# A planned four-layer graph network on one core: where the attention weights are turned, who issues the loads, and how the last layer's products are split

## The chip, the cores and the metric

The kernel runs on one core of a Trainium2 chip. The metric is the device time of one execution in microseconds; the kernel before took 2353.08 us (median of three runs, 2349.69 to 2353.46).

## What is computed

Four pre-norm layers over 128 graphs of 128 nodes with 256 features each, in float32, with a 0/1 adjacency matrix `adj` for every graph. Before every layer h = relu(layernorm(x)); the layer's result is added to x.

```python
# layer 0: gated graph network, three steps with the same GRU weights
for i in range(3):
    m = einsum('bnd,de->bne', h, weight[i])
    h = gru_cell(einsum('bst,bsd->btd', A, m), h, w_ih, w_hh, b_ih, b_hh)
x = x + h
# layer 1: relational convolution (with a 0/1 adj only relation 1 is present)
x = x + (adj == 1) @ h @ weight[0] + bias
# layers 2 and 3: graph attention
Wh = h @ W.T
e = leaky_relu(Wh @ a1 [:, None] + Wh @ a2 [None, :], 0.2), masked by adj
x = x + softmax(e) @ Wh
```

## The kernel before

**Groups.** The 128 graphs are worked through in 32 groups of G = 4 graphs (`group`, L918). A tile of a group holds 128 partitions by T = 512 columns of float32, which is one PSUM bank. Groups 0 to 29 treat their four graphs in one piece (`whole`); the last two are split into pairs and single graphs (SPLIT, SINGLE), to shorten the end.

**Layer 0.** `norm` takes statistics (L696), computes 1/sqrt on GpSimd (L722) and scales on ScalarE (L743). The features are turned, so that h stands with features on the partitions (`turn`, L478). Each of the three steps (`step`, L940) does the neighbour sum on TensorE (`gather`, L974), splits its operands into three parts (`forms`: a rounded part L955 or L957, a remainder L961 and their difference, `difference` L470, mostly on GpSimd), and multiplies them with split weights in fp32r passes (`products`, L992). Between the passes ScalarE or VectorE rescales the bank (L1005, L1011, L1013). The gates are finished by L1023, L1035, L1040, L1042, L1045 and L1048. After each step h is turned back. The last step's h is added to x by `residual` (L1078 to L1083); the planner puts each addition on VectorE or on GpSimd.

**Turning over DRAM.** `turn` lets VectorE transpose blocks of 32 by 32 (L490), stores the tile in a DRAM buffer (`give`, L493, on SP), and loads it back with blocks exchanged, in four transfers (`take`, L502, on SP). TENSOR names what is turned by TensorE instead; before it is empty.

**Layers 1 to 3.** `product` (L792) multiplies first with the adjacency or the attention weights (`sums`, L765) and then with the layer's weight. If the layer is in THIN and the group is not one of the last PLAIN = 2, the intermediate bank is split in three forms (L806 or L808, L811, L470) and the second product is made of fp32r passes (`passes`, L819) with one rescale (L828 or L830) before the third. Otherwise the bank is copied (`evict`, L461) and multiplied in plain f32 (`mix`, L775). Before, THIN is (1, 2): layer 3 is plain. In attention (`attend`, L1129) the scores e are built and masked (L1119, L1166, L1170, L1173), exponentiated (L1179), turned (`turn`, in whole groups) into eT, and eT enters `product`; L1210 adds the normalized result to x.

**Loads.** Every group loads x twice (`fetch`, L510, two transfers each time), adj twice (`load`, L529, and `again`, L522) and the transposed adj once (L1095), each by SP. The first weights are issued by ScalarE's queue, the others by SP (`weights`, L540). Results are stored by SP (L1220).

**Order of the work.** The order on every engine is written out ahead by a planner (`Plan.order`, L215). It holds for each operation an engine or a choice of engines, a planned duration (`act`, `dve`, `dma` and numbers in the calls), and what it depends on. It places the operation that can start first, and among the operations of an engine that can start within NEAR the one with the lowest rank. The rank is made of the group's turn (PERIOD per group), the length of the way that still follows, and an offset per stage and site (OFFSETS). AHEAD = 5 groups may be open at a time. Buffers are counted: 8 PSUM banks, 11 `big` tiles, 3 of x, 5 of adjacency and others. Engines run their own lists in order and wait on semaphores.

Of the kernel before, what the change touches and what calls it, by code (L numbers as in the profile page):

```python
# [18 lines left out]
P = 128  # L19
# [19 lines left out]
OWN = {"PE": 0, "ACT": 125, "DVE": 125, "POOL": 80, "SP": 2500, "ACTQ": 2500}  # L39
PERIOD = 29902  # L40
CLOSE = 7183
CLOSING = 2
SOON = -210
# [3 lines left out]
LINE, SPREAD = 0, -1000  # L47
GIVE = -400
TAKE = -2500
TENSOR = ()  # L50
BLOCK = 32
NEAR = 69
# [12 lines left out]
THIN = (1, 2)  # L65
# [11 lines left out]
def act(n, ptrs=0):  # L77
    return 50 + 95 * ptrs + 0.833 * n


def dve(n):
    return 68 + n / 0.96


def dma(kb):
    return 470
# [3 lines left out]
    0: (-70252, -12514, 2287, 8809, -26238, -146194, 10750, 55634, 30994, -54821, -2879, -215, -254,),  # L90
    1: (-77596, -18751, -40109, -33244, -13055, -53723, -68528, 1773, -34806, -135119, 879, -98768, 51856,
        44795, -64452, -2716,),
    2: (-95804, -20611, 70568, -66959, -6282, -38365, 6331, 7167, -87557, -120685, 144159, 0, -60172, 22200,
        253, 2907, 38047,),
    3: (-102445, -23990, 38859, 16506, -38395, -77755, 61821, 576, 58832, 37279, 38392, 48590, -137270, -161,
        -4329, 88294, -5659, -1511, -24936, -35483,),
    4: (9420, 6970, 96990, 45577, 14137, -3081, -28597, -108133, -850, -77398, -8748, -81, 24213, -39147,
        5274, -117520, -39070, 4328, 73461, 2677, -9322, 38218,),
    5: (-53063, -10484, 13614, 9709, -9223, 0, 86360, -49387, 3891, -79089, 22834, -12125, 42, -143071,
        -20815, -7001, 39402, 8197, 210921, 979, -8129, 55104, -109511, 178418, -171023, -17919, -45955,  # L100
        32785, 202299, 15929, -75290, -16189,),
    6: (-8401, 1876, 0, -2867, -17545, -54409, -177384, 6635, -4173, 16809, 64025, 1422, -41374, 3498, 7298,
        112681, -960, 0, -167733, 3047, -20901, 48681, -50794, 104147, -14530,),
    7: (2011, -43268, -7473, -2193, -13120, 17374, 10030, 24727, -8835, -59753, 29500, -32772, -10542,
        -85496, -6214, -47593, 4322, -5746, -43839, -101654, -3101, 9392, -18883,),
    10: (31340, 140410, 166041, 86764, 86271, -82403, 47762, 173067, 157481, -33091, 90840, -8460, 85813,),
    11: (-90811, -5747, -11338, -10756, 2168, -27498, -36330, -9110, 13623, -65824, 59954, -36485, 65854,
        102114, -39462, 10659,),
    12: (-88894, -2718, 120398, -47746, 16864, -33143, 17060, 25017, -58235, -111482, 170409, 89873, -65258,
        61044, 3422, 23111, 49690,),  # L110
    13: (-59071, 17894, 109447, 41927, -4268, -51312, 111328, 77067, 108356, 88471, 46360, 263340, -35253,
        23414, 79162, 211888, 10834, -10383, 74698, 67176,),
    14: (-32758, 12684, 122607, -43352, -20519, -34186, -56784, -88737, -18648, -122741, -24236, -29303,
        31876, -49287, -17477, -128202, -71886, 71670, 64769, 11212, -103569, -34527,),
    15: (-186417, -106904, -40789, -64266, -8033, -13445, 16411, -115394, -129609, -221523, -34547, -153159,
        -40482, -146129, -99541, -93701, -50044, 14115, 99121, -155460, -34394, 49772, -135635, 90451,
        -238640, -50117, -75732, -67304, 110359, -120923, -153053, -106347,),
    16: (90192, 31519, 28924, 59971, 13927, -108659, -126696, 35607, 7022, 44259, 134646, 83504, 72967,
        -71833, 139898, 214088, -4475, 66727, -178916, 46932, 84371, 67621, 13000, 119832, 93548,),
    17: (2011, -43268, -7473, -2193, -13120, 17374, 10030, 24727, -8835, -59753, 29500, -32772, -10542,  # L120
        -85496, -6214, -47593, 4322, -5746, -43839, -101654, -3101, 9392, -18883,),
    20: (-107741, -75380, -118420, -44708, -69924, -229335, -95079, 10513, -7484, 27055, -96949, -215, -254,),
    21: (-241039, -37443, -85617, -204164, -130954, -212658, -180409, -165567, -39823, -261311, -133885,
        -103620, -20641, -66103, -225402, -138454,),
    22: (-120431, -90137, 129948, -127092, 11177, -90000, -80347, -35815, -106293, -139261, 141530, -54256,
        -129233, 7860, -119111, 29072, 3576,),
    23: (-144176, -87227, -85789, 1378, -81324, -238467, -3162, -78700, 46997, -3871, 33809, 42358, -177604,
        -35904, -119077, -63937, -38348, -135903, -24936, -35483,),
    24: (-200969, -199448, -70412, -199813, -160146, -250664, -235592, -342997, -205357, -303708, -186137,
        -202706, -168399, -243146, -236370, -300082, -270699, -214705, -104544, 2677, -9322, 38218,),  # L130
    25: (-61251, -50204, -55609, -84828, -90010, 10545, -51986, -177143, -111208, -144284, 59013, -46623,
        -56779, -179794, -83802, -190091, -64080, -63359, 54466, -41363, -72589, -54011, -140205, 135055,
        -306980, -77123, -140787, 32785, 202299, 15929, -75290, -16189,),
    26: (-81589, -13318, 8156, -109205, -83353, -110277, -231535, -35494, -89897, 10694, 20288, -77730,
        -166910, -72981, -43136, 895, -48027, -102602, -242066, -114463, -91143, 43689, -72571, 104147,
        -14530,),
    27: (2011, -43268, -7473, -2193, -13120, 17374, 10030, 24727, -8835, -59753, 29500, -32772, -10542,
        -85496, -6214, -47593, 4322, -5746, -43839, -101654, -3101, 9392, -18883,),
# [235 lines left out]
def kernel(  # L374
# [49 lines left out]
    def build(general):  # L424
# [53 lines left out]
        def turn(nm, srcs, dst=None, w=None):  # L478
# [7 lines left out]
            for k, (src, r) in enumerate(srcs):  # L486
                part = chunk(f"part{nm}{k}")

                def within(src=src, part=part):
                    nc.vector.transpose(part.t, src())  # L490

                def give(k=k, part=part):
                    nc.sync.dma_start(out=swap.t[k * G : (k + 1) * G].rearrange("g p c -> p g c"),  # L493
                                      in_=part.t.rearrange("p (g c) -> p g c", g=G))

                op("DVE", dve(T) + 15, within, r=[r], w=[part])
                op("SP", 470, give, r=[part], w=[(swap, {k})], late=GIVE)
# [7 lines left out]
            op("SP", 470 * P // BLOCK, take, r=[swap], w=[w], late=TAKE)  # L505
# [3 lines left out]

        def fetch(gi, name, after=()):  # L510
            xt = Buf(xs, f"{name}{gi}")
            for g2 in range(G // 2):
                op("SP", dma(256), lambda g2=g2: nc.sync.dma_start(
                    out=xt.t[:, 2 * g2 : 2 * g2 + 2, :],
                    in_=x[ds(gi * G + 2 * g2, 2)].rearrange("g n d -> n g d")),
                   w=[(xt, {2 * g2, 2 * g2 + 1})], after=after)
            return xt
# [4 lines left out]
        def again(gi, after):  # L522
            ai = Buf(adjs, f"again{gi}")
            op("SP", dma(256), lambda: nc.sync.dma_start(
                out=ai.t.rearrange("p (g j) -> p g j", g=G),
                in_=adj[ds(gi * G, G)].rearrange("g i j -> i g j")), w=[ai], after=after)
            return ai

        def load(gi):  # L529
            xt, ai = fetch(gi, "x0_"), Buf(adjs, f"adj{gi}")  # L530
            op("SP", dma(256), lambda: nc.sync.dma_start(
                out=ai.t.rearrange("p (g j) -> p g j", g=G),
                in_=adj[ds(gi * G, G)].rearrange("g i j -> i g j")), w=[ai])
            state[gi] = xt, ai
# [383 lines left out]
        def group(gi):  # L918
# [21 lines left out]
            def step(i, hs, hT):  # L940
# [136 lines left out]
                for k, h in enumerate(hs_new if i == L - 1 else ()):  # L1077
                    def residual(eng, k=k, h=h):  # L1078
                        part = xt.t[:, :, k * P : (k + 1) * P]
                        (nc.gpsimd if eng == "POOL" else nc.vector).tensor_tensor(  # L1080
                            part, part, h.t.rearrange("p (g d) -> p g d", g=G), ALU.add)

                    op(("DVE", "POOL"), (dve(T), 1250), residual, r=[h], w=[(xt, set(range(G)))], port=True)  # L1083
# [3 lines left out]
            for i in range(L):  # L1087
# [7 lines left out]
            op("SP", dma(256), lambda: nc.sync.dma_start(  # L1095
                out=aiT.t.rearrange("p (g j) -> p g j", g=G),
                in_=adjT[ds(gi * G, G)].rearrange("g i j -> i g j")), w=[aiT], after=late)
# [12 lines left out]
            def attention(i, mask):  # L1110
# [4 lines left out]
                for g in range(G):  # L1115
# [9 lines left out]
                    op("DVE", 850, terms, r=[(hs[g // 2], {g}), ub[i]], w=[junk, (s, {("ei", g)})], port=True)  # L1125
# [159 lines left out]
```

## Time and profile before

| | |
|---|---|
| runs | 2353.08, 2349.69, 2353.46 us |
| profiled execution | 2353.06 us, its span 2351.2 us |
| L992, GRU products | 6912 instructions, means 396 and 393 ns |
| L974 and L765, neighbour sums | 3072 instructions, means 276 to 278 ns |
| L775, plain f32 second products | 576 instructions, means 380 and 407 ns |
| L819, fp32r passes | 1440 instructions, means 294 and 285 ns |
| L490, 32x32 turns on VectorE | 252 of h and 60 of e, means 697 and 693 ns |
| L1080, last h added | 47 on VectorE (870 ns), 13 on GpSimd (1315 ns) |
| loads issued by SP | x 128, adj 64, transposed adj 32, of 256 KB each |
| swap stores and loads issued by SP | 312 of 256 KB; 992 of 64 KB and 128 of 128 KB |
| DMA | 270.36 MB, mean 115 GB/s |

A row of the groups gives the line of the kernel, the engine, the operation, the tiles written and read, their shape, how many there were, their busy time and the mean of one. A matmul's duration reaches from its first row to its last result, so consecutive ones overlap. A row of waits gives the waiting engine and line, the engine and line it waited for, the sum in us, how many times, and the longest.

### The profile page before, as it was taken

The numbers are of one execution on the slowest core, as the hardware profiler recorded it, in microseconds if no ns is written. First come the engines' busy times: TensorE is split into PE (matmuls) and PEld (weight loads), VectorE is DVE, ScalarE is ACT, GpSimd is POOL, SyncE is SP. The second block draws the span as 40 slices with busy tenths as digits, with TensorE's granted clock in tenths as the row PEclk, the third lists the DMA queues.
The fourth block names the chain that finished last, engine by engine and source line by source line (L and its number), as shares of the span: only waits on it lengthen the run. The fifth ranks groups of instructions, "written<-read, shape, count | busy, mean of one in ns | idle before, by whom it ended". The sixth has DMA issues, their size and how long they took to land.

```text
span 2351.2 us, 39064 instructions
## 1 busy us (share of the span) xinstructions
PE 2291.9 (97%) x12137; PEld 1947.2 (83%) x12137; DVE 1978.2 (84%) x5405; ACT 1582.0 (67%) x3272; POOL 912.4 (39%) x729
## 2 busy tenths in 40 slices
PE   7999999999999999999999999999999999999997
PEld 6788888888888888888888888888888888788885
DVE  7858888888888888888888888888888888888887
ACT  6566676766676666666666766666766666666665
POOL 2334334443334443334343334343334343344421
PEclk9999999999999999999999999999999999999999
DMA  8535445555445455455455455455554555545431
GB/s 249 143 83 110 96 90 124 117 128 116 102 110 125 111 133 113 100 117 117 114 126 118 107 115 115 114 129 116 108 115 112 118 122 109 128 103 118 105 77 43
DMA packets 951273, 270.36 MB, mean 115 GB/s; under 512 B 677008, under 2 KB 939280, under 8 KB 951056
## 3 DMA queue, kind: packets, MB, share of 16 engines
q1 hardware_dynamic: 949968, 266.72, 50.0%
q8 instruction: 99, 1.62, 0.3%
q14 instruction: 118, 0.97, 0.2%
q10 hardware_dynamic: 1088, 1.05, 0.1%
HBM read 168.96 MB, written 98.69 MB: 114 GB/s over the span
## 4 chain that ended last, share of the span: by engine, by line
PE 64%; DVE 14%; DMA 10%; ACT 6%; SPq 4%; issue 3%; DVEq 0%; POOL 0%; ACTq 0%
PE bank L992 40%; PE bank L819 7%; PE bank L765 6%; PE bank L974 5%; PE bank L775 5%; DMA swap<-big 4%; SPq L502 4%; DMA big<-swap 3%; DVE junk L1119 3%; DVE form L961 2%; DMA wide<-swap 2%; ACT big L743 1%; DVE wide L1042 1%; DVE wide L1045 1%; DVE big L490 1%
## 5 line engine op out<-in xcount | busy, mean ns | idle before, releaser
L992 PE MATMUL bank<-form,wh_s 128*128 128x512 f32 x3456 | 953.4, 396 | 8.7 <-ACT bank L1005 4.6
L992 PE MATMUL bank<-form,wi_s 128*128 128x512 f32 x3456 | 944.0, 393 | 1.6 <-ACT bank L1013 0.9
L470 POOL TENSOR_TENSOR form<-form,form 128x512 fp32r<-128x512 f32 x383 | 517.7, 1362 | 800.4 <-DVE form L961 565.0
L992 PEld LDWEIGHTS bank<-form,wi_s 128*128 128x128 f32 x3456 | 644.1, 188 | 143.6 <-ACT bank L1013 3.1
L992 PEld LDWEIGHTS bank<-form,wh_s 128*128 128x128 f32 x3456 | 631.8, 188 | 151.5 <-ACT bank L1005 15.8
L1013 ACT ACTIVATE bank<-bank 128x512 f32<-128x512 f32 x448 | 255.4, 574 | 325.7 <-PE bank L992 324.4
L722 POOL TENSOR_TENSOR small<-small,nhalf 128x4 f32<-128x4 f32 (+2 forms) x140 | 142.2, 1020 | 408.8 <-DVE small L720 338.9
L1119 DVE CUSTOM_DVE_ANT_0 junk<-big,ub 128x256 bf16<-128x256 f32 x512 | 244.5, 478 | 14.2 <-ACT big L743 0.5
L743 ACT ACTIVATE big<-xs,small 128x256 f32<-128x256 f32 x384 | 200.1, 590 | 21.6 <-DVE small L726 12.2
L696 DVE BATCH_NORM_STATS2 small<-xs 128x6 f32<-128x256 f32 x512 | 190.0, 415 | 7.3 <-DMA xs<-in_x_dram 6.0
L470 POOL TENSOR_TENSOR cform<-cform,cform 128x512 fp32r<-128x512 f32 x120 | 155.2, 1294 | 96.2 <-DVE cform L811 83.0
L490 DVE STREAM_TRANSPOSE big<-wide 128x512 f32<-128x512 f32 x252 | 173.1, 697 | 4.0 <-ACT wide L743 2.3
L1035 DVE SCALAR_TENSOR_TENSOR bank<-big,bank 128x512 f32<-128x512 f32 x192 | 131.9, 690 | 48.5 <-PE bank L992 35.9
L955 ACT ACTIVATE form<-wide 128x512 fp32r<-128x512 f32 x179 | 109.2, 626 | 83.7 <-DMA wide<-swap 43.4
L1179 ACT ACTIVATE big<-big,small 128x128 f32<-128x128 f32 x256 | 99.8, 392 | 70.0 <-DVE small L1173 69.7
L1023 ACT ACTIVATE bank<-bank,b_rz 128x512 f32<-128x512 f32 x192 | 123.4, 655 | 34.0 <-PE bank L992 30.1
L1210 DVE SCALAR_TENSOR_TENSOR xs<-bank,small,xs 128x256 f32<-128x256 f32 x256 | 118.4, 475 | 31.6 <-PE bank L775 23.0
L1042 DVE TENSOR_TENSOR wide<-wide,bank 128x512 f32<-128x512 f32 x192 | 126.9, 682 | 21.4 <-ACT bank L1040 21.1
L765 PE MATMUL bank<-big,big 128*128 128x128 f32 x1024 | 130.7, 277 | 11.9 <-DVE wide L1045 7.1
L1023 ACT ACTIVATE big<-bank,b_rz 128x512 f32<-128x512 f32 x192 | 130.1, 681 | 16.3 <-PE bank L992 12.1
L765 PEld LDWEIGHTS bank<-big,big 128*128 128x128 f32 x1024 | 123.1, 192 | 19.4 <-DVE wide L1045 9.9
L974 PE MATMUL bank<-adjs,big 128*128 128x128 f32 x1024 | 131.2, 276 | 6.4 <-DMA big<-swap 5.1
(105 smaller groups left out, 3297.5 us busy)
## 6 DMA issues: line engine op xcount, KB each, us to landing
swap<-big SPq DMA_DIRECT2D x312, 256.0 KB, 2.5
big<-swap SPq DMA_DIRECT2D x992, 64.0 KB, 2.3
xs<-in_x_dram SPq DMA_DIRECT2D x128, 256.0 KB, 3.1
adjs<-in_adj_dram SPq DMA_DIRECT2D x64, 256.0 KB, 3.4
wide<-swap SPq DMA_DIRECT2D x128, 128.0 KB, 3.6
big<-line SPq DMA_DIRECT2D x60, 256.0 KB, 3.9
out_dram<-xs SPq DMA_DIRECT2D x30, 512.0 KB, 3.1
big<-in_adj_dram SPq DMA_DIRECT2D x32, 256.0 KB, 4.0
```

Source lines behind the costliest of these rows:

```text
L470: (nc.gpsimd if eng == "POOL" else nc.vector).tensor_tensor(at(df), at(lo).bitcast(F32), at(hi).bitcast(F32), ALU.subtract)
L490: nc.vector.transpose(part.t, src())
L696: op("DVE", dve(D), lambda g=g: nc.vector.bn_stats(s.t[:, ST + 6 * g : ST + 6 * g + 6], xt.t[:, g, :]), r=[(xt, {g})], w=[(s, {("mv", g)})])
L743: nc.scalar.activation(place(g), xt.t[:, g, :].rearrange("p (k m) -> p k m", k=KC), AF.Relu, bias=s.t[:, MR + g : MR + g + 1], scale=s.t[: ...
L765: nc.tensor.matmul(ps.t[:, (len(gs) * k + j) * P : (len(gs) * k + j + 1) * P], hs[g // 2].t[:, (g % 2) * D + k * P : (g % 2) * D + (k + 1) ...
L819: nc.tensor.matmul(po.t[:, j * D : (j + 1) * D], fs[f].t[:, (len(gs) * k + j) * P : (len(gs) * k + j + 1) * P], w.t[:, f, k, :], start=(st ...
L974: nc.tensor.matmul(pg.t[:, g * P : (g + 1) * P], of()[:, g * P : (g + 1) * P], flags(m0)[:, g * P : (g + 1) * P], start=True, stop=True,)
L992: nc.tensor.matmul(ps.t, w.t[(slice(None), *row, j, k, slice(c * P, (c + 1) * P))], b.t, start=(start and x == 0), stop=(x == len(terms) - ...
L1013: nc.scalar.mul(ps.t, ps.t, by)
L1023: op("ACT", act(T, 1), lambda: nc.scalar.activation(to.t, ps.t, AF.Tanh, bias=b_rz.t[:, c : c + 1], scale=0.5), r=[b_rz, *([ps] if kept el ...
L1042: op("DVE", dve(T), lambda c=c, ps=ps: nc.vector.tensor_tensor(hT.t[:, c, :], hT.t[:, c, :], ps.t, ALU.subtract), r=[ps], w=[(hT, {c})])
L1119: nc.vector.tensor_tensor_reduce(out=junk.t, in0=part, in1=ub[i].t[:, v, :], op0=ALU.mult, op1=ALU.add, scale=1.0, scalar=0.0, accum_out=s ...
```

## The change

- TENSOR becomes `("e",)`: in whole groups, too, the attention weights are turned by four TensorE transposes into a bank and copied out (`turn_all` and `evict`, which the last groups used before).
- A helper `arrive` issues the loads of x, adj and transposed adj by ScalarE (QUEUE = "ACT"), in ScalarE's own list of work.
- THIN becomes (1, 2, 3): layer 3's second product is made in three passes as well, with split weights.
- `residual` is always on GpSimd.
- The planner's durations, margins, PERIOD, CLOSE and all OFFSETS have other values, so the order of the work is another one.

```diff
-OWN = {"PE": 0, "ACT": 125, "DVE": 125, "POOL": 80, "SP": 2500, "ACTQ": 2500}
-PERIOD = 29902
-CLOSE = 7183
+OWN = {"PE": 0, "ACT": 125, "DVE": 125, "POOL": 80, "SP": 4500, "ACTQ": 2500}
+PERIOD = 31654
+CLOSE = 21692
 CLOSING = 2
-SOON = -210
+SOON = -3057
...
-LINE, SPREAD = 0, -1000
-GIVE = -400
-TAKE = -2500
-TENSOR = ()
+LINE, SPREAD = -1800, -1400
+GIVE = -2500
+TAKE = -2600
+TENSOR = ("e",)
+ISSUE = 530
+LANDING = 4400
+QUEUE = "ACT"
 BLOCK = 32
-NEAR = 69
+NEAR = 72
...
-THIN = (1, 2)
+THIN = (1, 2, 3)
...
 def act(n, ptrs=0):
-    return 50 + 95 * ptrs + 0.833 * n
+    return 57 + 95 * ptrs + 0.833 * n
 def dve(n):
-    return 68 + n / 0.96
+    return 74 + n / 0.96
 def dma(kb):
-    return 470
+    return ISSUE
...
-                op("SP", 470, give, r=[part], w=[(swap, {k})], late=GIVE)
+                op("SP", ISSUE, give, r=[part], w=[(swap, {k})], late=GIVE)
...
-            op("SP", 470 * P // BLOCK, take, r=[swap], w=[w], late=TAKE)
+            op("SP", ISSUE * P // BLOCK, take, r=[swap], w=[w], late=TAKE + 800 * (n - 1))
...
+        def arrive(dst, src, w, after=()):
+            on_act = QUEUE == "ACT"
+            op(QUEUE, dma(256), lambda: (nc.scalar if on_act else nc.sync).dma_start(out=dst(), in_=src), w=w,
+               after=after, late=LANDING if on_act else 0)
...
-                op("SP", dma(256), lambda g2=g2: nc.sync.dma_start(
-                    out=xt.t[:, 2 * g2 : 2 * g2 + 2, :],
-                    in_=x[ds(gi * G + 2 * g2, 2)].rearrange("g n d -> n g d")),
-                   w=[(xt, {2 * g2, 2 * g2 + 1})], after=after)
+                arrive(lambda g2=g2: xt.t[:, 2 * g2 : 2 * g2 + 2, :],
+                       x[ds(gi * G + 2 * g2, 2)].rearrange("g n d -> n g d"), [(xt, {2 * g2, 2 * g2 + 1})], after)
...
-                    def residual(eng, k=k, h=h):
+                    def residual(k=k, h=h):
                         part = xt.t[:, :, k * P : (k + 1) * P]
-                        (nc.gpsimd if eng == "POOL" else nc.vector).tensor_tensor(
-                            part, part, h.t.rearrange("p (g d) -> p g d", g=G), ALU.add)
-                    op(("DVE", "POOL"), (dve(T), 1250), residual, r=[h], w=[(xt, set(range(G)))], port=True)
+                        nc.gpsimd.tensor_tensor(part, part, h.t.rearrange("p (g d) -> p g d", g=G), ALU.add)
+                    op("POOL", 1250, residual, r=[h], w=[(xt, set(range(G)))], port=True)
...
-                    op("DVE", 850, terms, r=[(hs[g // 2], {g}), ub[i]], w=[junk, (s, {("ei", g)})], port=True)
+                    op("DVE", 880, terms, r=[(hs[g // 2], {g}), ub[i]], w=[junk, (s, {("ei", g)})], port=True)
```

The loads of adj (`again`, `load`) and of the transposed adj use `arrive` in the same way.

## The prediction

> **What bounds the kernel now.** I read the page first: engine shares, then the slices.
>
> ```profile
> span 2351.2 us, 39064 instructions
> PE 2291.9 (97%) x12137; PEld 1947.2 (83%) x12137; DVE 1978.2 (84%) x5405; ACT 1582.0 (67%) x3272; POOL 912.4 (39%) x729
> ...
> PE   7999999999999999999999999999999999999997
> ...
> PEclk9999999999999999999999999999999999999999
> ```
>
> TensorE is busy 97% of the span and near full clock everywhere except at both ends. The page warns that matmul ends are modelled, so I looked at starts, in the timeline of PE alone, in two stretches of the middle.
>
> ```profile
> 1205.10 1.89 PE L775 MATMUL bank<-wa,big 128*128 128x256 f32 x8
> 1206.64 1.30 PE L819 MATMUL bank<-w_s,cform 128*128 128x256 f32 x8
> 1207.77 1.89 PE L775 MATMUL bank<-wa,big 128*128 128x256 f32 x8
> ...
> 1211.84 1.09 PE L819 MATMUL bank<-w_s,cform 128*128 128x256 f32 x8
> 1212.77 1.08 PE L992 MATMUL bank<-form,wi_s 128*128 128x512 f32 x4
> 1213.68 0.62 PE L992 MATMUL bank<-form,wh_s 128*128 128x512 f32 x2
> ...
> 1214.60 0.64 PE L819 MATMUL bank<-w_s,cform 128*128 128x256 f32 x4
> 1215.09 0.39 PE L992 MATMUL bank<-form,wh_s 128*128 128x512 f32 x1
> ```
>
> Start to next start gives what an instruction really takes of the stream. Four L992 take 1213.68 - 1212.77 = 0.91 us (0.229 each). Eight L819 take 0.93 (0.117 each), four 0.49. Eight L775 and eight L819 take 1207.77 - 1205.10 = 2.67, so eight L775 take 2.67 - 0.93 = 1.74 (0.217 each). The 128-column products of L765 and L974 step by 0.112. Summed over the counts of the groups: 6912 x 0.229 + 3072 x 0.112 + 1440 x 0.118 + 576 x 0.217 + about 20 for the rest = 2242 to 2250 us. The last matmul starts at 2345. So about 100 us in all are gaps: about 26 in the first 100 us, 29 after 2250, and only some 45 to 50 in the 2150 us between, 2%. Any change that adds matmuls adds time nearly one for one; anything else can only move the gaps. Which gaps, the waits of PE's weight loads and matmuls say:
>
> ```profile
> PEld bank L992 <- ACT bank L1005: 15.8, 26, 1.4
> PEld bank L992 <- DVE form L961: 10.1, 25, 0.9
> PEld bank L765 <- DVE wide L1045: 9.9, 14, 1.7
> ...
> PEld bank L992 <- ACT bank L1013: 5.9, 16, 1.3
> ...
> PEld bank L775 <- ACT big L461: 4.8, 8, 0.9
> ...
> PE bank L974 <- DMA big<-swap: 5.1, 8, 1.5
> ...
> PE bank L765 <- DMA big<-swap: 3.9, 6, 1.6
> ```
>
> They are many short waits, shared between ScalarE (about 27 us with the small rows), VectorE (about 26) and turned tiles from DRAM (about 11 with PEld's own 2.0).
>
> **The change, part by part.** Sums stand against the profiled execution, 2353.06 us (span 2351.2 and 1.9 around it); the median, 2353.08, is the same number.
>
> *Three passes in the last layer too.* It holds for groups 0 to 29, two pairs each: 60 pairs. Eight L775 go (four f32 products, each issued as two instructions; 1.74 us), twelve L819 come (0.93 + 0.49 = 1.42): -0.32 x 60 = **-19 us** of TensorE. The two layers that have it already show what waits the passes bring: the named waits of L819, PE's and PEld's, add to 4.9 us for 120 pairs, so +2.4 for 60. Beside it: one copy L461 (0.66 on DVE, 0.59 on ACT) is replaced by a rounding L806 (ACT 0.595), a remainder L811 (DVE 0.679), a difference L470 (POOL 1.294) and a rescale L830 (ACT 0.583 in 97 of 120 cases). Splitting the weights once costs ten instructions of about 0.41 us and they are not needed before the last layer of group 0; it lies in the first 100 us, where PE waits anyway. I take 0, at most 4. One more plain copy of that weight is loaded for the last two groups and holds one of 11 big tiles near the end: 0, at most 2.
>
> *Attention weights on TensorE.* Sixty times (two attentions, 30 groups), four transposes replace a VectorE 32x32 turn (L490, 0.693), one store and four loads of SP (0.377 + 4 x 0.486 = 2.3 us of its queue) and the flight through DRAM (2.5 and 2.3 us to landing). The last groups already do it; the timeline shows what four transposes of this form take:
>
> ```profile
> 2296.29 0.60 PE L1061 MATMUL bank<-ident,wide 128*128 128x128 f32 x4
> 2296.72 0.50 PE L765 MATMUL bank<-big,big 128*128 128x128 f32 x3
> ```
>
> 0.43 us from first start to the next product, so 60 x 0.43 = **+26 us**. Here the Trainium skill speaks more strongly against the change: "TensorE: Matmul & The Clock Gate", section "Part 4: PE-mode transpose", puts a 128x128 transpose at about 275 ns in one kernel's context, which would be 240 x 0.275 = 66 us and a total about 40 higher. The groups' own mean for L1061 is 276 ns too, but that is first row to last result; the starts are 0.108 apart, since the instructions overlap. In a full stream the row decides: I take 26, keep 30 as the upper end (an isolated four may expose its first weight load) and 24 as the lower. Each four also needs a PSUM bank and an eviction (0.59 ACT or 0.66 DVE), some 1.3 us of a bank each; with the three-pass banks held about 2.7 us longer per pair this is 60 x (1.3 + 2.7) = 240 us of 8 x 2350 bank-us, 1.3%: 0 to 4 us of waits, inside the round figure below.
> What goes: waits for the e tiles in the rows of L765 from swap, 3.9 + 2.0: **-6 us** (0 to -6: those rows contain only 8 waits, and what is late next is the exponential L1179, which then releases the transposes).
>
> *Loads issued by ScalarE.* 128 loads of x and 96 of the flags, 224, leave SP. On ACT each takes its issue time out of an in-order engine that also does L1005, L1013, L955. The three weight loads issued by ACT at the start took 1.57 us, 0.52 each; SP's own medians for these loads are 0.39 to 0.50. So 224 x 0.5 = 112 us (87 to 117). None is hidden from ACT's queue, but ACT has 33% idle time, so it is paid only as waiting for ACT. SP gains the same and 139 us from the turns; SP mostly waits for work (L493 for VectorE's turns, 371 us), so that is worth nothing by itself. At the start up to three loads stand before the weights that PE awaits at 6.3 us: 0 to +1.5, I take +1.
>
> *Last h added by GpSimd.* 47 of 60 additions leave VectorE: 47 x 0.87 = 41 us, and the waits that stand in front of them:
>
> ```profile
> DVE xs L1080 <- DMA big<-swap: 66.5, 45, 3.3
> ```
>
> On GpSimd the sum costs 1.315 instead of 0.69 to 0.87, and the same DMA wait now stands before L470 (differences), for which PE's third pass waits. GpSimd goes to 912 + 60 x 1.294 + 47 x 1.315 = 1052 us, 45%; PE's waits for L470 are 1.4 us now. Bounds -1 to +5; I take +1. bn_stats of the next norm sees x 0.5 us later, 60 times; with five groups in flight I take 0.
>
> *Loads of the engines, and so the gaps.* ACT: 1582 + 35.7 (rounding) + 28.3 (rescale) + 112 = 1758, 67.3% to 74.8%; the eT evictions replace the c evictions. Waiting in a queue grows roughly like u/(1-u): 2.06 to 2.97, so ACT's 27 us become 39: **+12**. DVE: 1978 - 41.6 (turns) - 40.9 + 40.7 (L811) + 8 (rescale share) = 1945, and 66 us of blocked time go; 86.9% to 82.7% by the same rule makes 26 us into 19: **-7**. This is the softest step; by the rates alone each could be between 0 and twice that. The order of all work is planned anew (all offsets, margins and the closing weights differ): no row prices that. The gaps of the middle are 48 us and those at the ends 55; I let the new order move them by -25 to +25, with 0 taken.
>
> Sum: -19 + 2.4 + 26 - 6 + 1 + 1 + 12 - 7 = +10.4; 2353.06 + 10.4 = **2363 us**.
>
> **The rivals.** *Gaps shrink.* VectorE is freed of 107 us of work and blocked time, the DRAM path of a fifth of its stores, and big tiles are held shorter. If that halves the middle gaps: +9 matmul and passes, -24: 2338. For it: 66.5 us of blocked VectorE, and L961, L1045 among PE's waits. Against it: ACT's rows weigh as much and ACT gets 176 us more, and no PE row is long (1.7 at most).
> *ScalarE held by a load* (slower). A load waits for its tile: SP now waits 120.6 us at L513 for ACT and 69.9 for the store out_dram<-xs, 25 times, 2.8 on average. If on ACT such a wait stands before L1013 or L955, PE runs on for about 1 us (a ready bank or two, 4 L992 are 0.91), then stops: 25 x 1.8 = 45 us at worst; with half of the loads put late enough, +23: 2353 + 9 + 23 = 2385. It decides from about five waits over 2 us on. Against it: SP is an engine with little else to do, so its waits do not show that those tiles are late for the plan, and the planner books 4.5 us for a store.
> *Nothing measurable.* Matmul time +7 and gaps -7: 2353. In particular the moved loads may do nothing, as they are early: waits for x are 6.0 us in the whole trace, and for flags under 4.
>
> **How the numbers follow.** The measurement can tell about 0.2% from no change, 4.7 us: 2348.4 to 2357.8. Forecast 2363 (own range 2351 to 2374): 0.47, of which 0.08 falls inside 0.2%. Gaps shrink, 2338: 0.32, of which 0.02 inside. ScalarE held, 2385: 0.10. Nothing measurable: 0.11, of which 0.01 below. That gives faster 0.31, same 0.20, slower 0.49. For 8 in 10 the range reaches into both rivals: 2332 (the shrunk gaps) to 2386 (ACT held, or the rule's doubled waits).
>
> **What would show it.** PE: L775 falls from 576 to the 96 of the last two groups, L819 rises from 1440 to 2160, 240 more transposes at L1200, starts about 0.11 apart; the sum of starts 7 us longer. ACT near 1755 counting issues (some 1650 as the page counts), and its rows in PE's waits above 35 us. DVE near 1945, L1080 only on POOL. Waits of ACT for its own loads' tiles under 20 us. Wrong if transposes step by 0.2 or more (+24), if PE's waits fall below half (the faster rival), or if ACT waits at L513 for stores with PE idle behind (the slower).

## The result and the profile after

The changed kernel takes 2404.8 us (median of four runs, 2399.4 to 2408.4), against 2351.4 for the kernel before: ratio 1.0224, 95% interval 1.0204 to 1.0244. It is slower by some 53 us, where +10 was forecast and 2386 was the top of the range. In the table of experiments all times are ratios to the kernel before on the same chip; 0.1% is 2.3 us.

The profiled execution spans 2397.6 us, 46.4 more than before. First its page (line numbers of the changed kernel: L992 is L998, L974 is L980, L819 is L825, L502 is L507, L1080 is L1086).

```profile
span 2397.6 us, 39392 instructions
PE 2310.4 (96%) x12617; PEld 1969.6 (82%) x12617; DVE 2044.4 (85%) x5442; ACT 1617.7 (67%) x3321; POOL 1052.2 (44%) x833
...
PE 56%; DVE 26%; DMA 9%; ACT 4%; SPq 3%; issue 2%; POOL 0%; DVEq 0%; ACTq 0%; POOLq 0%
...
xs<-in_x_dram ACTq DMA_DIRECT2D x128, 256.0 KB, 3.5
```

TensorE is still at 96%, but in the chain that ended last it has lost eight points (64% before) and VectorE has gained twelve (14% before). VectorE's busy time rose by 66 us, where I had it fall by 33. One part are choices of the planner: 75 rescales of three-pass products stand on VectorE (23 before) and 26 of their roundings (2 before), 52 us more together. That it moved them because the loads are charged to ScalarE is my reading. Another 47 us are operations of the same shape and number that took longer: the score sums L1119, the minimum L1173 and the operation at L1170. The last section returns to them.

The starts of the matmuls, summed by kind as in the prediction (0.229, 0.112, 0.118, 0.217 or 0.109 us each), give 2253.0 us of TensorE work against 2245.6: +7.4, the term of the prediction. The other 39 of the 46.4 us are time beyond these steps, called gaps here. Placed in time: first 100 us, 26.3 to 31.3; from 100 to 2200, 49.1 to 74.2; after that 24.7 to 33.7. In the middle the gaps before the neighbour sums (L974, now L980) rose from 4.9 to 39.2 us, those before the three-pass products from 3.8 to 17.8, those before the GRU products fell from 24.9 to 12.1, and those before the sums of layers 1 to 3 (L765, now L771) from about 15 to under 1. The waits of PE say the same (`swap` is the DRAM buffer through which a tile is turned):

```profile
PE bank L980 <- DMA big<-swap: 32.2, 27, 4.0
...
PE bank L825 <- DVE cform L817: 6.9, 11, 1.3
```

Before, that first row read 5.1 us. It now comes 27 times, about once per group of four graphs, with a median of 1.0 us. One of these places, in SP's and PE's timelines:

```profile
1241.36 0.95 SPq L498 DMA_DIRECT2D swap<-big  x2
1243.75 4.85 SPq L507 DMA_DIRECT2D big<-swap  x8
```

```profile
1248.07 0.71 PE L825 MATMUL bank<-w_s,cform 128*128 128x256 f32 x4
1249.63 1.13 PE L980 MATMUL bank<-adjs,big 128*128 128x128 f32 x8 [0.85 <-DMA big<-swap]
```

SP stores the two turned halves of h and issues their eight loads. TensorE, done at 1248.78, needs the first four, which land at 1245.66, 1246.82, 1248.16 and 1249.38. The third and the fourth take 3.0 and 3.7 us from the end of their issue. Two loads of x, issued by ScalarE at 1244.59 and 1245.17, are in flight until 1247.90 and 1249.12.

Not all of the gaps are waits. The clock granted to TensorE was halved for 13.7 us in the middle (2025.5 to 2032.3 and 2107.4 to 2114.3 us); in the kernel before it was full from 44.4 to 2304 us. In both places it fell during one of the two longest waits for a turned tile:

```profile
2026.54 2.05 PE L980 MATMUL bank<-adjs,big 128*128 128x128 f32 x8 [2.45 <-DMA big<-swap]
...
2029.24 1.91 PE L998 MATMUL bank<-form,wh_s 128*128 128x512 f32 x4
2030.95 1.73 PE L998 MATMUL bank<-form,wi_s 128*128 128x512 f32 x4
...
2108.92 2.05 PE L980 MATMUL bank<-adjs,big 128*128 128x128 f32 x8 [4.02 <-DMA big<-swap]
```

Four L998 take 2030.95 - 2029.24 = 1.71 us there, 0.427 each instead of 0.229. After 2200 us the halved time is 22.6 us against 11.7. My estimate, half of the time in which matmuls ran at the halved clock: 6.6 us lost before, 17.0 after (5.6 of it in the middle, 8.1 after 2200). So about 10 of the 39 us are a slower TensorE. The prediction had no term for that. Whether the late tiles brought the clock down was not tested.

The transposes are as costed: L1204's median step from start to start is 0.108 us. ScalarE's 224 issues take 0.418 us on average (93.5 in all), no wait of ScalarE before an issue shows more than 17 ns, and the longest issue took 0.80 us: the slower rival of the prediction, a load that holds ScalarE, did not happen.

### The profile page after: what moved, and what is told of

Its sections match the earlier page's. It is cut to its first block, busy times and chain, and to the rows that moved or that the text cites. A ratio compares the mean times of both kernels' runs of the same rounds, so it can differ in the third digit from the quotient of the medians.

```text
span 2397.6 us, 39392 instructions
## 1 busy us (share of the span) xinstructions
PE 2310.4 (96%) x12617; PEld 1969.6 (82%) x12617; DVE 2044.4 (85%) x5442; ACT 1617.7 (67%) x3321; POOL 1052.2 (44%) x833
## 3 DMA queue, kind: packets, MB, share of 16 engines
q1 hardware_dynamic: 706336, 176.77, 33.7%
## 4 chain that ended last, share of the span: by engine, by line
PE 56%; DVE 26%; DMA 9%; ACT 4%; SPq 3%; issue 2%; POOL 0%; DVEq 0%; ACTq 0%; POOLq 0%
PE bank L998 36%; PE bank L825 8%; DVE junk L1123 5%; PE bank L980 5%; PE bank L771 5%; DMA big<-swap 4%; DVE form L967 3%; SPq L507 3%; DVE wide L1048 2%; DMA swap<-big 2%; DVE wide L1054 2%; DVE wide L1051 2%; DMA big<-line 2%; DVE small L702 2%; DVE big L495 2%
## 5 line engine op out<-in xcount | busy, mean ns | idle before, releaser
L998 PE MATMUL bank<-form,wi_s 128*128 128x512 f32 x3456 | 953.2, 395 | 5.2 <-ACT bank L1019 2.6
L998 PE MATMUL bank<-form,wh_s 128*128 128x512 f32 x3456 | 947.7, 396 | 4.9 <-ACT form L961 4.5
L998 PEld LDWEIGHTS bank<-form,wi_s 128*128 128x128 f32 x3456 | 639.8, 189 | 141.8 <-ACT bank L1019 4.9
L998 PEld LDWEIGHTS bank<-form,wh_s 128*128 128x128 f32 x3456 | 626.5, 189 | 122.4 <-ACT form L961 4.7
L1019 ACT ACTIVATE bank<-bank 128x512 f32<-128x512 f32 x469 | 272.9, 582 | 315.2 <-PE bank L998 272.7
L475 POOL TENSOR_TENSOR cform<-cform,cform 128x512 fp32r<-128x512 f32 x178 | 231.7, 1302 | 238.1 <-DVE cform L817 183.6
L728 POOL TENSOR_TENSOR small<-small,nhalf 128x4 f32<-128x4 f32 (+2 forms) x140 | 151.0, 1080 | 362.3 <-DVE small L726 338.1
L1123 DVE CUSTOM_DVE_ANT_0 junk<-big,ub 128x256 bf16<-128x256 f32 x512 | 267.5, 522 | 12.8 <-ACT big L749 0.3
L825 PE MATMUL bank<-wa,cform 128*128 128x256 f32 x1440 | 217.8, 287 | 8.1 <-DVE cform L817 6.4
L825 PEld LDWEIGHTS bank<-wa,cform 128*128 128x128 f32 x1440 | 194.3, 189 | 33.5 <-DVE cform L817 13.7
L980 PE MATMUL bank<-adjs,big 128*128 128x128 f32 x1024 | 139.8, 280 | 34.3 <-DMA big<-swap 32.2
L980 PEld LDWEIGHTS bank<-adjs,big 128*128 128x128 f32 x1024 | 128.7, 193 | 44.0 <-issue 31.4
L961 ACT ACTIVATE form<-bank 128x512 fp32r<-128x512 f32 x143 | 85.0, 598 | 113.2 <-PE bank L980 109.6
L967 DVE SCALAR_TENSOR_TENSOR form<-form,bank 128x512 fp32r<-128x512 f32 x192 | 130.2, 681 | 31.8 <-ACT form L961 30.8
```

What stands on the lines that cost most here:

```text
L475: (nc.gpsimd if eng == "POOL" else nc.vector).tensor_tensor(at(df), at(lo).bitcast(F32), at(hi).bitcast(F32), ALU.subtract)
L728: op("POOL", 1000, lambda: nc.gpsimd.tensor_tensor(columns(RS), columns(RS), nhalf.t[:, gs.start : gs.stop], ALU.pow), r=[nhalf], w=[own(" ...
L825: nc.tensor.matmul(po.t[:, j * D : (j + 1) * D], fs[f].t[:, (len(gs) * k + j) * P : (len(gs) * k + j + 1) * P], w.t[:, f, k, :], start=(st ...
L967: op("DVE", dve(T), lambda: nc.vector.scalar_tensor_tensor(lo.t, f(hi), -1 / UNIT, src(), ALU.mult, ALU.add), r=[dep, hi, token], w=[lo], ...
L980: nc.tensor.matmul(pg.t[:, g * P : (g + 1) * P], of()[:, g * P : (g + 1) * P], flags(m0)[:, g * P : (g + 1) * P], start=True, stop=True,)
L998: nc.tensor.matmul(ps.t, w.t[(slice(None), *row, j, k, slice(c * P, (c + 1) * P))], b.t, start=(start and x == 0), stop=(x == len(terms) - ...
```

## The experiments

My theory after the result was that the new order of work itself has more waits; rivals were the loads on ScalarE (by its time, or by their way through the DMA engines), GpSimd's additions, and the added operations. Names that begin with b keep the order of the kernel before, those with a that of the changed kernel: an operation is only changed in its place, so that nothing is planned anew, unless it is said.

| kernel | ratio to before | 95% interval |
|---|---|---|
| changed kernel | 1.0224 | 1.0204 to 1.0244 |
| b_loads_act | 1.0079 | 1.0059 to 1.0099 |
| b_add_pool | 1.0054 | 1.0037 to 1.0070 |
| a_loads_sp | 1.0130 | 1.0108 to 1.0152 |
| a_add_dve | 1.0264 | 1.0240 to 1.0288 |
| b_near72 (planned anew) | 1.1439 | 1.1412 to 1.1466 |
| b_thin3 (planned anew) | 1.1451 | 1.1419 to 1.1483 |
| b_e_pe (planned anew) | 1.1101 | 1.1072 to 1.1131 |
| b_act_held | 1.0018 | 1.0010 to 1.0026 |
| a_sp_held | 1.0145 | 1.0125 to 1.0164 |
| a_loads_short | 1.0093 | 1.0077 to 1.0110 |
| a_sp_short | 1.0094 | 1.0078 to 1.0111 |
| b_short | 0.9996 | 0.9989 to 1.0003 |
| a_no_turn | 1.0204 | 1.0176 to 1.0232 |
| a_sp_no_turn | 1.0114 | 1.0097 to 1.0130 |
| a_l3_plain | 1.0275 | 1.0258 to 1.0292 |
| a_sp_terms | 1.0106 | 1.0082 to 1.0129 |
| b_terms | 0.9921 | 0.9898 to 0.9945 |
| a_sp_flex_act | 1.0155 | 1.0128 to 1.0181 |

**Who issues the loads.** b_loads_act and a_loads_sp change one word:

```diff
# b_loads_act, at the four loads of x, adj, adj again and transposed adj
-nc.sync.dma_start(
+nc.scalar.dma_start(
# a_loads_sp, in arrive
-(nc.scalar if on_act else nc.sync).dma_start(
+nc.sync.dma_start(
```

> The kernel before with its own order of work; only the 224 loads of x and the flags are issued by ScalarE, at their old places in the list. If ScalarE's issuing is what costs (224 x 0.42 us = 94 us in an in-order engine, before the rescales that PE waits for), the time rises by 15 to 45 us over before's 2351. If the loss lies in the new order of work, it rises by 0 to 8 us.

> The changed kernel with its own order; the loads are issued by SP again, at the same places. If ScalarE's issuing costs, the time falls by 20 us or more from 2405. If the new order of work is to blame, it falls by at most 10 us.

Measured +0.79% (18.5 us) in the old order and -0.94% (22 us) in the new one. The order is fixed in each, so this much is the loads' issuing engine, and my first theory was at best part of it. In b_loads_act the same row grew as in the changed kernel (5.1 before):

```profile
PE bank L974 <- DMA big<-swap: 15.6, 19, 3.0
```

In the new order it goes the other way less clearly: PE's row falls from 32.2 to 24.3 in a_loads_sp, while all gaps of the middle fall from 74.2 to 57.3. Some 4 us of the 20 in its profile lie in the first 100 us: TensorE's first matmul starts at 9.0 us in the changed kernel and at 6.4 in a_loads_sp. In the old order it is 8.8 against 6.3, and 6 of the 14 us by which the profile of b_loads_act is longer than that of before lie in the first 100.

**ScalarE's time, or the way through the DMA engines.** Two kernels keep the loads on SP and only occupy ScalarE in their places, by a copy of 128x256 (0.398 us each) and by two small copies:

```diff
# b_act_held
+            load()                             # nc.sync.dma_start
+            nc.scalar.copy(idle.t, idle.t)     # 128 x 256
# a_sp_held
+nc.sync.dma_start(out=dst(), in_=src), nc.scalar.copy(idle), nc.scalar.copy(idle)   # 128 x 4 each
```

> The kernel before with its own order and its loads on SP; behind every load's place ScalarE also copies a scratch tile of 128x256 (about 0.4 us, 224 times), which nobody waits for. It shows the time of ScalarE alone. If the loads on ScalarE cost by holding its list, this costs the same 15 to 22 us as b_loads_act. If they cost by mixing with the turned tiles in the DMA engines (or by waits for their tiles), this costs under 8 us.

> The changed kernel with its own order and the loads issued by SP at their places; in the place of each load ScalarE makes two small copies of a scratch tile (together about 0.4 us, as long as an issue). If what costs in the loads on ScalarE is ScalarE's time, it is as slow as the changed kernel (1.022 of before). If it is the mixing of loads with turned tiles in the DMA engines, it stays near the changed kernel with loads on SP (1.013), at most 1.016.

They cost +0.18% over before and +0.15% over a_loads_sp (intervals overlapping): about 4 us. Each adds some 70 us to ScalarE's busy time, where the issues take 94. So ScalarE's time is about a fifth of the loss and not the loss. Two more kernels take away the bytes instead and keep every issue (from group 4 on; the rest of x is left out):

```diff
-arrive(lambda: xt.t[:, 2 * g2 : 2 * g2 + 2, :], x[...])
+arrive(lambda: xt.t[:, 2 * g2 : 2 * g2 + 2, :32], x[...][:, :, :32])
```

> The changed kernel, loads on ScalarE as in it, but from group 4 on a load of x moves only 32 of 256 columns (it leaves the rest of x out; everything else is computed on what is there). Issues and order are the same, the bytes of x an eighth. If the mixing in the DMA engines costs, it wins back a good part of the 22 us: 8 to 18 below the changed kernel (1.015 to 1.019). If ScalarE's time or the order costs, it stays at 1.022.

> The changed kernel with its own order, loads issued by SP, and from group 4 on only 32 of 256 columns of x loaded (the rest of x is left out). If mixing in two queues is what costs, the bytes on SP's own queue are nearly free: 0 to 5 us below the changed kernel with loads on SP (1.011 to 1.013). If the traffic itself costs wherever it is issued, it falls like the short loads on ScalarE did, to 1.002 to 1.006.

> The kernel before with its own order and loads on SP, and from group 4 on only 32 of 256 columns of x loaded (the rest of x is left out). If traffic from SP's own queue is nearly free, 0 to 5 us below before (0.998 to 1.000). If the traffic itself costs, 10 us or more below (under 0.996).

With short loads the new order takes 1.0093 from ScalarE's queue and 1.0094 from SP's: once the bytes are gone, the issuing engine no longer matters. With full loads it was 1.0224 and 1.0130. So what the second queue costs in the new order hangs on the bytes of x. The trace shows where they meet the turned tiles. For every load from swap (`take`) issued between 40 and 2200 us, the table has the mean time from the end of its issue to its landing. It is given for those that had a load of x or flags in flight at any time from their issue to their landing, for those that had none, and for those that had one already in flight when their own issue ended ("ahead"). The last column is the mean time of the four takes of one tile, from the first issue to the last landing.

| kernel | with, us (count) | without, us (count) | ahead, us (count) | four takes, us |
|---|---|---|---|---|
| changed kernel, loads on ScalarE | 2.66 (350) | 2.11 (493) | 2.89 (276) | 4.43 |
| a_loads_sp | 2.10 (368) | 2.08 (484) | 2.38 (174) | 4.04 |
| a_loads_short | 2.19 (326) | 2.06 (528) | 2.36 (229) | 4.10 |
| a_sp_short | 1.90 (338) | 2.04 (513) | 1.94 (124) | 3.95 |
| before | 2.13 (282) | 1.99 (796) | 2.50 (110) | 3.96 |
| b_loads_act | 2.30 (155) | 1.97 (919) | 2.71 (77) | 4.06 |

One queue does not keep the two apart. The first column hides it, since in SP's queue it also counts loads issued behind the take. Where a full load is ahead, the take lands late from SP's queue too: 2.38 us in a_loads_sp and 2.50 in before, where all other takes need 2.01 and 1.97. From ScalarE's queue it is later (2.89 and 2.71, against 2.07 and 1.97 for the others), and in the new order it happens oftener (276 takes against 174). The Trainium skill states in "DMA: Bandwidth & Descriptors", section "Issuing engines are not separate DMA queues", that whatever engine issued them, transfers run on the same 16 DMA engines and interleave. The delays from both queues agree with it; why a load from the second queue delays a take more, no run here shows.

These means do not carry the whole account. In a_loads_short the four takes need no less than in a_loads_sp (4.10 and 4.04 us), and yet it is faster by 0.4% (the intervals just overlap), with 15 us of gaps before L980 against 30. Which tile is late counts, and a mean does not tell that. In the old order the four takes lengthen by only 0.1 us. There some 6 us of the loss lie in the first 100 us and up to 4 in ScalarE's time, so the delay of turned tiles can be about half of it.

b_short adds that in the old order the loads' traffic costs nothing from SP's queue (0.9996); in the new one it still costs 0.36% (the intervals just overlap).

**The addition on GpSimd.**

```diff
# b_add_pool: always nc.gpsimd.tensor_tensor; a_add_dve: always nc.vector.tensor_tensor
```

> The kernel before with its own order; only the 47 additions of the last h that VectorE made are made by GpSimd at the same places. If the addition on GpSimd, with its wait for the turned tile, holds up the differences and so PE's third pass, the time rises by 10 us or more. If the new order is to blame, it stays within 5 us of before.

> The changed kernel with its own order; the 60 additions of the last h are made by VectorE at the same places. If GpSimd's additions cost (its 147 us of waits for turned tiles, before the differences), the time falls by 10 us or more from 2405. If the new order is to blame, it stays or rises by up to 15 us, since VectorE then stands in that wait.

The old order is slower with all additions on GpSimd (+0.54%). The new one is not clearly slower with all of them on VectorE (+0.40%, intervals overlapping). So a forced addition on GpSimd shows no loss in the order that was made for it, and costs 12.7 us in the one that was not. There VectorE then waits for GpSimd:

```profile
DVE small L696 <- POOL xs L1080: 81.6, 25, 5.2
```

**What the order is worth.** b_near72 changes one planner number (NEAR, 69 to 72), b_thin3 only THIN and b_e_pe only TENSOR. Each is planned anew with the offsets of before; in the last two these are spread over a changed list of operations.

> The kernel before with one number of the planner changed, NEAR 69 to 72, and so the same work in another order: the measure of what a new order costs by itself. If a tuned order can be replaced at no cost, it stays within 5 us of before's 2346. If the order is worth something by itself, it is slower by 10 us or more.

> The kernel before with three passes in layer 3 too, planned anew with before's numbers and offsets (the new operations take those of the ones they replace). By matmul time -19 us; if the passes bring few waits, -10 to -17 against before. If the new order eats it, between -5 and +20.

> The kernel before with the attention weights turned by TensorE, planned anew with before's numbers. By matmul time +26 us, less up to 6 of waits for the turned weights: +20 to +27. If the transposes step by 0.275 us[...], +60. If the new order costs too, +30 to +45.

The same work in an order that differs by 3 ns of a planner's margin takes 14.4% longer, 337 us. Its page:

```profile
PE 2403.3 (90%) x12137; PEld 2011.4 (75%) x12137; DVE 2001.2 (75%) x5374; ACT 1593.9 (60%) x3265; POOL 966.4 (36%) x767
```

TensorE has the same 12137 instructions and 10% idle time: the offsets do not fit even this neighbouring order. Idle time is not all of it. The mean granted clock is 0.946 (0.996 before), and TensorE's busy time for the same instructions rose from 2291.9 to 2403.3 us. By the same estimate as above some 80 of the 337 us are matmuls at the halved clock. This makes b_thin3 and b_e_pe useless for their question: their +14.5% and +11.0% are the price of an untuned order, not of the three passes or the transposes. It also means that, with all offsets replaced, the two kernels compared here are two separately made orders, and that a part of the change can only be priced in place.

**The transposes and the three passes in place.**

```diff
# a_no_turn (and a_sp_no_turn, with the loads on SP): groups 0 to 29
-for g in gs: nc.tensor.transpose(at(pp, g), at(e, g), ident.t)
-evict(N, ..., lambda: pp.t[:, :N])
+evict(N, ..., lambda: e.t[:, :N])
# a_l3_plain, layer 3: no remainder, difference, rescale
-passes((0, 1)); scale; passes((2,))      # 12 fp32r matmuls a pair
+mix with fs[0] and w.t[:, 0, k, :]       # 8 instructions of plain f32
```

> The changed kernel with its own order, without the 240 transposes of the attention weights in groups 0 to 29: the copy takes e as it is (the turning is left out). If TensorE's stream is paid one for one, it is 26 us faster (1.011 to 1.012). If the transposes' waits for the exponentials (12 us in the rows of the changed kernel) come on top, up to 38 faster; if the gaps come back elsewhere, 5 to 20.

> The changed kernel with its own order, loads issued by SP, and without the 240 transposes (the turning of the attention weights is left out). If the mixed loads set the period and TensorE is the bound once they are gone, it is 20 to 26 us faster than the changed kernel with loads on SP (1.002 to 1.005). If the new order has another bound of its own, it gains only 0 to 10 us (1.009 to 1.013).

> The changed kernel with its own order; layer 3 of groups 0 to 29 multiplies its rounded part once in plain f32 with the rounded part of the weights (remainder, difference, rescale and the second and third parts are left out). TensorE gets 19 us more; VectorE, ScalarE and GpSimd lose 41 + about 35 + 78 us. If matmul time decides, it is about 19 us slower than the changed kernel less its few waits (1.026 to 1.030). If the three passes cost by their waits on VectorE and GpSimd (18 us of gaps before the passes now), it is equal or faster (1.015 to 1.022).

Without 240 transposes TensorE has 26.2 us less to do, and the kernel is 0.20% (4.7 us) faster with the loads on ScalarE and 0.16% (3.7) with the loads on SP; the intervals of each pair overlap. The gaps take the rest: in the middle they rise from 74.2 to 91.0 us, and a row that grows is the one of the three-pass products (6.9 in the changed kernel):

```profile
PE bank L825 <- DVE cform L817: 18.6, 18, 2.5
```

a_l3_plain, the other way, puts 18.7 us of matmul time in and is 0.5% (12 us) slower; its middle gaps fall from 74.2 to 63.8. That lies in the range expected if matmul time decides (1.026 to 1.030), although this kernel also takes work from the other three engines. So in the new order TensorE's stream is paid in part: at most 4 to 5 of 26 us for the transposes, about 12 of 19 for the three passes of layer 3.

**A second bound.** VectorE was the candidate, by its share of the chain.

```diff
# a_sp_terms, b_terms: the score sums of attention over 32 of 256 features (the rest left out)
-in0=part, in1=ub[i].t[:, v, :]
+in0=part[:, :32], in1=ub[i].t[:, v, :32]
# a_sp_flex_act: the three-pass rescale and rounding always on ScalarE
```

> The changed kernel with its own order, loads issued by SP, and VectorE lightened by some 150 us: the score sums of attention (L1123) run over 32 of 256 features (the rest is left out). If VectorE is the second bound of the new order, it falls by 12 us or more below the changed kernel with loads on SP (under 1.008). If its list only has other places of waiting, 0 to 6 us (1.0105 to 1.013).

> The kernel before with its own order and the same shortened score sums (the rest of the features is left out). If TensorE is the only bound there, 0 to 8 us below before (0.9965 to 1.000). If VectorE holds this order as well, 12 us or more below (under 0.995).

> The changed kernel with its own order, loads issued by SP, and at their places the 75 rescales and 26 roundings of the three-pass products that the planner had put on VectorE are made by ScalarE. VectorE gets 70 us less, ScalarE 60 us more. If VectorE's load is what costs, 5 to 15 us below the changed kernel with loads on SP (1.0065 to 1.011). If not, the same or up to 10 us slower.

The answer is the reverse of what I expected. In the old order VectorE is a second bound: 121 us less of its work (1978.2 to 1857.4 busy) make the kernel 18.5 us faster, and TensorE's middle gaps fall from 49.1 to 20.4. Some 20 of these 29 us stood before the GRU products, so it is not only the shorter chain of attention itself:

```profile
PE 2275.4 (98%) x12137; PEld 1949.7 (84%) x12137; DVE 1857.4 (80%) x5405; ACT 1590.1 (69%) x3272; POOL 906.7 (39%) x729
```

In the new order the same saves 5 to 6 us (1.0130 to 1.0106, intervals overlapping), and taking 69 us of rescales and roundings from VectorE (its busy time falls by 41) does not make it faster (1.0155, intervals overlapping). What stays in a_loads_sp, a_sp_no_turn, a_sp_terms and a_sp_flex_act is the wait for the turned halves of h, 30 to 37 us of middle gaps before L980:

```profile
PE bank L980 <- DMA big<-swap: 24.7, 34, 2.0
PE bank L825 <- DVE cform L817: 7.1, 14, 1.5
```

(a_sp_terms). Neither less TensorE work nor less VectorE work shortens that way, while fewer bytes of x do: in a_sp_short these gaps are 21.3 us, in a_loads_short 15.1. That the turned tiles' way through DRAM is the new order's second bound fits these runs; it is argued, not shown.

No kernel here that computes everything beats the one before.

## Why the prediction was wrong, point by point

Two steps failed. *By mechanism, the loads*: +13 us was forecast for them (+12 for waiting in ScalarE's queue, +1 for the head), 22 were measured in the new order. Only about 4 are ScalarE's time. The traffic beside the turned tiles, which I took at nothing, makes most of the rest. That 13 came as near to 22 as it did is luck. *By size, the rest of the sum*: without the loads it was -19 + 2.4 + 26 - 6 + 1 - 7 = -2.6 us, and a_loads_sp measured +30. Of the miss of 43 us, 33 stand here.

- **What bounds the kernel now**: right for before, and incomplete. TensorE's gaps were small, but b_terms shows that VectorE's load made about 29 of the 49 us in the middle. "Any change that adds matmuls adds time nearly one for one" failed for the changed kernel: 26 us of transposes are worth at most 4 to 5 there, and their intervals overlap.
- **Three passes**: the net term of matmul time, -19 + 26 = +7, was measured at +7.4. In place the three passes are worth 12 us instead of 19 less 2.4.
- **Attention weights**: the step of 0.108 us held (0.108), so the 275 ns of the Trainium skill ("TensorE: Matmul & The Clock Gate", section "Part 4: PE-mode transpose"), taken as a step, would have misled. The -6 for waits that go is not visible: fewer turned tiles are now waited for longer.
- **Loads issued by ScalarE**: I costed ScalarE's time (+12, measured about 4) and wrote that SP's gain and the moved transfers are worth nothing. I never asked what the loads would run beside once they were no longer in SP's queue. In the new order the four takes of a turned tile then need 4.43 us instead of 4.04, and the loads on ScalarE cost 22 us in all, some 40% of the whole loss; in the old order 18.5. The head, taken at +1, was about 4, and is part of it.
- **Last h on GpSimd**: +1, with bounds of -1 to +5. In the new order nothing is to be won by undoing it; in the old one it cost 12.7 us, outside the bounds.
- **Loads of the engines**: the sum for VectorE (-33 us, and from it -7 of waits) took the engine choices and the durations of before as fixed. The planner chose anew, and operations that ran beside GpSimd's work took longer; VectorE got +66. The queueing rule u/(1-u) predicted +12 from ScalarE's load and was three times too high.
- **The new order at 0, -25 to +25**: mis-sized. With the loads back on SP 1.30% remain, 30 us. The profile of a_loads_sp is 26 us longer than that of before: 7 are matmul time, about 11 the halved clock (4 in the middle, 8 after 2200 us, by the estimate above), and about 8 waits. So some 23 of the 30 fall to this term, within its range of 25, and neither the -6 nor the -7 was there to offset them. The size of the risk was far off too: b_near72 shows that an order can cost 337 us.
- **The rivals**: gaps did not shrink; ScalarE was not held by a load. Some 40% of the loss came through the same part of the change as in that rival, by another mechanism.

What stays open: how the remaining 30 us divide between the attention weights' new way, the end of the kernel and the fit of the offsets, whether the waits are what halves the clock, and which late tiles make up the loss. The first would take each variant with an order fitted to it, which was not tried; planned anew without that, each of the three tried loses 11% or more.

## What to carry to other kernels

Before moving transfers to another engine's queue, ask not only what the issuing costs but which short transfers they will then run beside: here 0.42 us of issue time was cheap, and 0.4 us more for a tile that another engine waits for was not. In a kernel whose order is written out ahead, price a part of a change in place, with the order kept, and measure once what a trivially different order costs. "TensorE is 97% busy" says where the stream is, not that each microsecond taken from it is won: check by leaving work out. And before calling the time between two matmuls a wait, look at the clock that was granted there.

## What the runs showed of the hardware

Three things were not expected.

- Loads of 256 KB that were already in flight lengthened the landing of 64 KB loads made of 128-byte packets: from 2.01 to 2.38 us out of the same queue (a_loads_sp), from 2.07 to 2.89 us out of another (changed kernel). The DMA engines were busy only 43% of the time in that stretch.
- VectorE operations that read two tiles took longer while GpSimd worked. The score sums L1119 took 422 ns on average where no GpSimd instruction of over 0.3 us ran beside them and 863 where one covered more than half of them (65 of 512); in the changed kernel it was 421 and 769 (149 of 512). That more of them met GpSimd is why their mean rose from 478 to 522 ns. Moving only the 47 additions to GpSimd (b_add_pool) raised the mean of the masked minimum L1173 from 299 to 464 ns.
- TensorE's clock was halved for 3.4 us or a few times that at once, in the middle of the changed kernel during waits of 2.4 and 4.0 us. The mean clock of 0.991 instead of 0.996 hides some 10 us.
